# A cross-attention block on one core: six products by seven blocks each, summed in chains in PSUM

## The chip, the cores and the metric

The kernel runs on one core of a Trainium2 chip. Its engines work side by side, each on its own queue in order: TensorE (PE) multiplies matrices into PSUM, an accumulator memory of eight banks of 512 numbers in each of 128 partitions; VectorE (DVE), ScalarE (ACT) and GpSimd (POOL) work element by element; SyncE (SP) here issues DMA transfers. The metric is the device time of one launch in microseconds, lower is better.

## The reference

128 sequences of 128 tokens with 256 features attend to a context of the same shape, with 16 heads of 16 features. Cut to what matters:

```python
q = (query @ Wq + bq); k = (key @ Wk + bk); v = (values @ Wv + bv)     # per head
scores = einsum('bhqd,bhkd->bhqk', q, k) / sqrt(16)
scores = where(j < i, scores, -1e30)             # key j before query i
attn = softmax(scores); attn[:, :, 0, :] = 0
x = layer_norm(query + (attn @ v) @ Wo + bo, ln1_g, ln1_b)
ffn = relu(x @ W1 + b1) @ W2 + b2                # 256 -> 1024 -> 256
out = layer_norm(x + ffn, ln2_g, ln2_b)
```

All of it is in 32-bit floating point. A matmul of that type is two instructions of the chip, each with its weight load.

## The kernel before

The 128 sequences go through in 64 pairs, 256 tokens a pair. A software pipeline, written out by hand, works on several pairs in one step: `step(p)` (L1475) holds the scores and exponentials of pair p, the queries and keys of p + 1, the weighting and output projection of p - 2, the first feed-forward product of p - 3 and the second one of p - 4, and the last normalisation of p - 5. Steps 2 to 6 have functions of their own (`third` to `sixth`), which fill the pipeline; steps 7 to 63 call `step`, and the lines from L1564 on drain it. The order in the code is the order of each engine's queue.

TensorE's part of a step, in its order: the weighting of values by probabilities in `weigh` (L534: 48 small matmuls at L544 and L554), the scores (L410), then four projections of 256 columns: queries (L270), attention output (L573), keys (L270) and values (L325). Each is four matmuls, so eight chip instructions. Then come the second feed-forward product (`second_by_seven`, L864) and the first (`hidden_by_seven`, L1450, of `Hidden`, L957), each split into two halves of its rows and columns and formed from seven block products in place of eight, after Winograd's form of Strassen's scheme. That takes sums of the input blocks (GpSimd, L859 to L862 and L952 to L955) and of the weight blocks (once, ahead), and gives products that are added up by VectorE (L903 to L926, L1002 to L1016). Each product by seven has 28 matmuls of 128 columns. `empty` puts TensorE instructions that do nothing behind a block; the second feed-forward product has 22 of them.

The low scores (queries 0 to 63 of a sequence) go to banks 6, 7, 4 and 5 and are masked into SBUF by `mask` (L419); the high ones stay in banks 0 to 3 and are masked in place (`mask_high`, L816). ScalarE takes the exponential head by head (L839) with the sum of each row as a second result. The sums' inverses are multiplied into the probabilities on GpSimd (`divide`, L482). The probabilities are then transposed in blocks of 32 x 32 on VectorE (`turn`, L491), and 16 transfers (`bring`, L504) carry the blocks to their partitions. The normed tokens are transposed likewise (`turn_x1`, L739) and go through DRAM in five transfers (`across`, L240). The buffers for probabilities, transposed blocks and carried blocks are four of one kind (`wide`, L358).

## Time and profile before

| | us |
|---|---|
| median of three runs | 1484.22 (1484.1 to 1484.62) |
| span of the profiled execution | 1482.7 |
| TensorE busy in it | 1475.0 |
| VectorE busy | 1386.3 |
| GpSimd busy | 1376.5 |
| ScalarE busy | 1324.1 |
| DMA | 204.63 MB, mean 138 GB/s |

The granted clock of TensorE is 0.999 over the span. Busy time counts overlapping instructions of an engine once; an instruction's length in the rows runs from its start to its end, and the next one can start before that end. A row of the chain of waits is a stretch of the chain that ended last; a row of the timeline is a run of like instructions, with the idle time of the engine before it and what released it in square brackets.

### The profile page before, as it was taken

How to read it: one execution, taken by the hardware profiler on the slowest of the kernel's cores; microseconds unless marked ns; L12 is line 12 of the kernel's file. 1: busy time of each engine (PE TensorE's matmuls, PEld its weight loads, DVE VectorE, ACT ScalarE, POOL GpSimd, SP SyncE). 2: the span in 40 equal slices, each digit the busy share in tenths (PEclk: the TensorE clock that was granted, in tenths of full speed). 3: DMA queues.
4: the chain of work that ended last, by engine and by line, in shares of the span. 5: the costliest groups of instructions: out<-in, count | busy, mean ns of one | idle time of the engine just before them, and what ended most of it. 6: DMA issues, size and time to landing. Idle time of an engine off the chain costs nothing.

```text
span 1482.7 us, 53916 instructions
## 1 busy us (share of the span) xinstructions
PE 1475.0 (99%) x19367; PEld 1378.1 (93%) x19367; DVE 1386.3 (93%) x2444; ACT 1324.1 (89%) x5272; POOL 1376.5 (93%) x1530
## 2 busy tenths in 40 slices
PE   9999999999999999999999999999999999999998
PEld 7788999999999999999999999999999999999998
DVE  7999999999999999999999999999999999999977
ACT  6668999999999999999999999999999999999963
POOL 6979999999999999999999999999999999999987
PEclk9999999999999999999999999999999999999999
DMA  8366666555655566665556556566655666555451
GB/s 201 79 133 150 148 150 141 127 146 138 154 144 133 138 146 138 149 144 130 144 132 156 146 128 143 144 137 150 145 132 141 136 153 148 128 141 131 109 137 51
DMA packets 415317, 204.63 MB, mean 138 GB/s; under 512 B 282448, under 2 KB 383056, under 8 KB 415056
## 3 DMA queue, kind: packets, MB, share of 16 engines
q1 hardware_dynamic: 412768, 199.34, 57.5%
q8 instruction: 160, 2.62, 0.8%
q10 hardware_dynamic: 2288, 1.85, 0.5%
q14 instruction: 101, 0.83, 0.2%
HBM read 70.26 MB, written 33.29 MB: 70 GB/s over the span
## 4 chain that ended last, share of the span: by engine, by line
PE 96%; DVE 2%; POOL 1%; ACT 0%; issue 0%; DMA 0%; POOLq 0%; DVEq 0%
PE banks L878 25%; PE banks L990 25%; PE banks L270 15%; PE banks L573 7%; PE banks L325 7%; PE banks L410 6%; PE banks L554 4%; PE banks L544 2%; PE banks L778 2%; PE banks L1042 0%; PE banks L797 0%; DVE su L468 0%; POOL sm L446 0%; PE banks L527 0%; POOL sm L470 0%
## 5 line engine op out<-in xcount | busy, mean ns | idle before, releaser
L839 ACT ACTIVATE sm<-banks,nmx 128x128 f32<-128x128 f32 x944 | 329.8, 377 | 16.3 <-DVE nmx L823 8.7
L485 POOL TENSOR_TENSOR sm<-sm,rs 128x1024 f32<-128x1024 f32 x171 | 322.6, 1901 | 0.0
L839 ACT ACTIVATE sm<-sm,nmx 128x64 f32<-128x64 f32 x944 | 312.5, 368 | 0.0
L497 DVE STREAM_TRANSPOSE tb<-sm 128x1024 f32<-128x1024 f32 x186 | 229.8, 1237 | 17.1 <-DMA pT<-tb 6.9
L1021 ACT ACTIVATE hT<-hT,b1e_c 128x256 f32<-128x256 f32 x464 | 198.1, 497 | 34.7 <-DVE hT L1009 21.0
L839 ACT ACTIVATION_READ_ACCUMULATOR sm<-sm,nmx 128x1 f32 x912 | 201.6, 221 | 0.0
L839 ACT ACTIVATION_READ_ACCUMULATOR sm<-banks,nmx 128x1 f32 x912 | 197.3, 216 | 0.0
L990 PE MATMUL banks<-xS,w1t 128*128 128x128 f32 x1392 | 174.4, 275 | 0.0
L878 PE MATMUL banks<-wt,hS 128*128 128x128 f32 x1440 | 170.7, 275 | 0.0
L878 PEld LDWEIGHTS banks<-wt,hS 128*128 128x128 f32 x1440 | 165.6, 192 | 0.1
L990 PEld LDWEIGHTS banks<-xS,w1t 128*128 128x128 f32 x1392 | 164.8, 192 | 0.0
L823 DVE TENSOR_REDUCE nmx<-banks 128x4 f32<-128x512 f32 x177 | 153.9, 869 | 6.0
L270 PE MATMUL banks<-xT,wq 128*128 128x256 f32 x504 | 125.4, 392 | 0.0
L315 ACT ACTIVATE kT<-banks,bkh,half 128x256 f32<-128x256 f32 x252 | 122.5, 590 | 2.8 <-PE banks L270 2.8
L990 PE MATMUL banks<-x1T,w 128*128 128x128 f32 x944 | 124.6, 275 | 0.2 <-DMA x1T<-x1t 0.2
L573 PE MATMUL banks<-wo,cxT 128*128 128x256 f32 x512 | 121.2, 379 | 0.0
L325 PE MATMUL banks<-wv,cT 128*128 128x256 f32 x512 | 121.0, 379 | 0.0
L270 PE MATMUL banks<-cT,wk 128*128 128x256 f32 x504 | 119.4, 380 | 0.1
L878 PEld LDWEIGHTS banks<-w,hT 128*128 128x128 f32 x944 | 114.7, 192 | 3.1
L990 PEld LDWEIGHTS banks<-x1T,w 128*128 128x128 f32 x944 | 114.9, 192 | 0.4 <-issue 0.3
L878 PE MATMUL banks<-w,hT 128*128 128x128 f32 x944 | 115.2, 275 | 0.0
L573 PEld LDWEIGHTS banks<-wo,cxT 128*128 128x128 f32 x512 | 97.0, 190 | 13.5 <-ACT cxT L566 0.3
(191 smaller groups left out, 3954.1 us busy)
## 6 DMA issues: line engine op xcount, KB each, us to landing
pT<-tb SPq DMA_DIRECT2D x976, 96.0 KB, 2.2
x1t<-tbx SPq DMA_DIRECT2D x252, 64.0 KB, 2.4
x1T<-x1t SPq DMA_DIRECT2D x63, 256.0 KB, 3.0
out_dram<-t SPq DMA_DIRECT2D x63, 256.0 KB, 3.1
xb<-in_x_dram SPq DMA_DIRECT2D x124, 128.0 KB, 3.7
cb<-in_ctx_dram SPq DMA_DIRECT2D x124, 128.0 KB, 4.2
x<-in_x_dram SPq DMA_DIRECT2D x31, 512.0 KB, 5.3
w<-in_L_xattn_W_dram SPq DMA_DIRECT2D x2, 1024.0 KB, 8.3
```

Of the source, the lines that this page charges most:

```text
L270: nc.tensor.matmul(ps[:, m * TP : (m + 1) * TP], w[:, k, m * P : (m + 1) * P], src[:, k, :], start=(k == 0), stop=(k == KC - 1),)
L315: nc.scalar.activation(st["kT"][:, m, e, :], pk[:, m * TP : (m + 1) * TP], AF.Identity, bias=bkh[:, m, e : e + 1], scale=half[:, e : e + 1],)
L325: nc.tensor.matmul(pv[:, s * D : (s + 1) * D], st["cT"][:, k, s * P : (s + 1) * P], wv[:, k, :], start=(k == 0), stop=(k == KC - 1),)
L410: nc.tensor.matmul(st["sps", hi][r][s * HP : (s + 1) * HP, m * 2 * n : (m + 1) * 2 * n].rearrange("p (e j) -> p e j", e=2), st["qT"][strip ...
L485: nc.gpsimd.tensor_tensor(sm[:, part, :], sm[:, part, :], st["rs", hi][:, part, None].to_broadcast([P, part.stop - part.start, sm.shape[2] ...
L497: nc.vector.transpose(st["tb"][:, :, at : at + 256].rearrange("p j (n a) -> p n j a", a=32), st["sm", hi].rearrange("p h j -> p (h j)")[:, ...
L573: nc.tensor.matmul(po[:, s * D : (s + 1) * D], cxT[:, k, s, :], wo[:, k, :], start=(k == 0), stop=(k == KC - 1),)
L823: nc.vector.tensor_reduce(st["nmx", 1][:, 4 * first : 4 * (first + n)], ps, AX.X, ALU.max, negate=True,)
L839: nc.scalar.activation(sm[:, h, :], src, AF.Exp, bias=nmx[:, h : h + 1], scale=1.0, **({"accum_out": st["su", hi][:, h : h + 1]} if summed ...
L878: nc.tensor.matmul(out, left(k), right(k), start=(k == 0), stop=(k == FC // 2 - 1))
L990: nc.tensor.matmul(ps[:, i * P : (i + 1) * P].rearrange("p (n a) -> p n a", a=32), left(i), right, start=True, stop=True,)
L1021: nc.scalar.activation(self.hT[:, f], self.plains.get(f, self.hT[:, f]), AF.Relu, bias=b1e_c[:, f : f + 1], scale=1.0,)
```

## The change

All six products of a step are now formed from seven blocks: queries, keys, values and attention output too, each with 7 matmuls of 128 columns (14 chip instructions) for the 4 of 256. Their input sums are made on GpSimd (`cc` for the context, which keys and values share, `xc` for the tokens, `oc` for the attention's context), the weight sums once in steps 5 and 6.

The seven blocks are summed in PSUM. A product has three accumulators of one bank (`a`, `b`, `f`; three banks for the first feed-forward product). Blocks 1, 2 and 5 start them; a reader on ScalarE or VectorE takes `a` and `f` out; blocks 6 and 3 are added onto `a` and `f`, a reader takes them out; then 7 onto `a`, a reader; then 4 onto `a`, a reader. A block is so held up until the reader ahead of it is through.

The probabilities are no longer divided on GpSimd. The inverses of the sums are transposed, each repeated 16 times (`turn_inverse`), and multiplied into the context where VectorE takes it out of PSUM, which ScalarE did before. One set of 16 transfers carries probabilities, inverses and the normed tokens of another pair; the way through DRAM goes in the steady steps. The buffers `turned` and `brought` are single, the probabilities' own (`wide`) too.

The step is a list of 151 names, `ORDER`, in place of nested calls; each engine takes its own names of it in that order. A name with -1 or -2 is run one or two passes later than its pair's other names: with -1 stand both feed-forward products (`w`, `h`) with nearly all that belongs to them, the low probabilities' and the inverses' turn; with -2 the rectifiers of the even hidden blocks (`re`), the odd ones' too (`ro`), and one half of the residual. Two passes are added behind step 62 to drain these, and `last_step` follows. `EMPTY` says how many empty TensorE instructions stand behind each group of blocks, 2 to 5. A pass has 768 TensorE instructions with its weight loads. The last normalisation is of pair p - 6. In steps 5 and 6 exponentials have their sums as second results, the weight sums of the projections are made, and the normed tokens and inverses are turned.

Names of the list that the next part uses: `weigh`, `scores`, `context`; `maskB3`, `maskB2`, `maskA` for the low scores, `add0` to `add3` and `max0` to `max3` for the high ones, one bank each; `eh` and `el` exponentials of two heads, high and low; `turn0` to `turn2` and `turni`; `o1` to `o4`, `v`, `q`, `k`, `w`, `h` the groups of blocks in a chain; `ok`, `oa`, `or` and the like their readers.

The diff, cut to its core:

```diff
-    def inverse(p, hi):
-        st = states[p]
-        rs = st["rs", hi] = small.tile([P, H], F32, tag=f"rs{hi}", name=f"rs{hi}_{p}")
-        nc.vector.reciprocal(rs, st["su", hi])
-
-    def divide(p, hi, part):
-        st = states[p]
-        sm = st["sm", hi]
-        nc.gpsimd.tensor_tensor(
-            sm[:, part, :], sm[:, part, :],
-            st["rs", hi][:, part, None].to_broadcast([P, part.stop - part.start, sm.shape[2]]),
-            ALU.mult,
-        )
+    def reciprocals(p):
+
+        st = states[p]
+        rs = st["rs"] = small.tile([P, 2 * H], F32, tag="rs", name=f"rs_{p}")
+        nc.vector.reciprocal(rs, st.pop("su"))
+
+    def turn_inverse(p):
+
+        st = states[p]
+        nc.vector.transpose(
+            turned[:, :, WIDTH : WIDTH + P].rearrange("p j (n a) -> p n j a", a=32),
+            st.pop("rs").rearrange("p (n g) -> p n g", n=4)[:, :, :, None].to_broadcast(
+                [P, 4, HH, DK]
+            ),
+        )
...
-    def bring(p, queue, which):
...
+    def bring(p, queue, which, whole=False):
+
+        blocks(p)
+        at = slice(p % 2 * P, p % 2 * P + ROW) if whole else slice(P, P + WIDTH)
         for u in which:
             i, j = u // NS, u % NS
             queue.dma_start(
-                st["pT whole"][32 * j : 32 * j + 32, i, :], st["tb"][32 * i : 32 * i + 32, j, :]
-            )
+                brought_all[32 * j : 32 * j + 32, i, at],
+                turned_all[32 * i : 32 * i + 32, j * ROW + at.start : j * ROW + at.stop],
+            )
...
+        if "inv" in states[p]:
+            parts = "p (m s l q a) -> p m s l q a"
+            pc = states[p].pop("pc").rearrange(parts, m=KC, s=2, l=2, q=2)
+            to = cxT.rearrange("p m s (l q a) -> p m s l q a", l=2, q=2)
+            inv = states[p].pop("inv")
+            nc.vector.tensor_tensor(
+                to[:, :, :, :, 1], pc[:, :, :, :, 1], inv[:, :, :, :, 1], ALU.mult
+            )
+            for l in range(2):
+                at = slice(1 - l, 32)
+                nc.vector.tensor_tensor(
+                    to[:, :, :, l, 0, at], pc[:, :, :, l, 0, at], inv[:, :, :, l, 0, at], ALU.mult
+                )
+            return
...
+    class Seven:
+
+        def __init__(self, at, data, sums, weights, mixed, turned=False, depth=1):
+            self.at, self.turned, self.depth = at, turned, depth
+            self.factors = {
+                1: (data(0, 0), weights(0, 0)), 2: (data(0, 1), weights(1, 0)),
+                5: (sums(0), mixed(0)), 6: (sums(1), mixed(1)), 3: (sums(3), weights(1, 1)),
+                7: (sums(2), mixed(2)), 4: (data(1, 1), mixed(3)),
+            }
+            self.name = f"pb{turns[0]}"
...
+        def run(self, *which):
+            for n in which:
+                out = self.of({2: 1, 5: 2, 3: 2}.get(n, 0))
+                left, right = self.factors[n]
+                if self.turned:
+                    left, right = right, left
+                for k in range(self.depth):
+                    nc.tensor.matmul(
+                        out, left(k) if self.depth > 1 else left,
+                        right(k) if self.depth > 1 else right,
+                        start=(n == 1 and k == 0), stop=(k == self.depth - 1),
+                        skip_group_check=True,
+                    )
...
+    class Onto(Seven):
+
+        def onto(self, t, base):
+            self.t = t.rearrange("p s (h d) -> p (s h) d", h=2)
+            self.base = base.rearrange("p s (h d) -> p (s h) d", h=2)
+
+        def join(self, to, src, of):
+            nc.vector.tensor_tensor(to, src, of, ALU.add)
+
+        def keep(self):
+            self.join(self.t[:, ::3], self.two(0, 2), self.base[:, ::3])
+
+        def keep2(self):
+            self.join(self.t[:, 1], self.a, self.base[:, 1])
+
+        def add(self):
+            self.join(self.t[:, 3], self.a, self.t[:, 3])
+
+        def add2(self):
+            self.join(self.t[:, :2], self.two(1), self.t[:, :2])
+
+        def rest(self):
+            self.join(self.t[:, 2], self.a, self.base[:, 2])
...
+    class First:
...
+        def run(self, *which):
+            raw = lambda s, k: self.x1T[:, s, :, k, :]
...
+                ps = self.banks[{2: 1, 5: 2, 3: 2}.get(n, 0)]
+                for i in range(NI):
+                    nc.tensor.matmul(
+                        ps[:, i * P : (i + 1) * P].rearrange("p (n a) -> p n a", a=32),
+                        left(i), right, start=(n in (1, 2, 5) and i == 0), stop=True,
+                        skip_group_check=True,
+                    )
...
+    KINDS = {
+        "V": (Values, 4), "O": (Attention, 5), "Q": (Queries, 7), "K": (Keys, 3),
+        "W": (Second, 6), "first": (First, 0, 2),
+    }
...
-    def hidden_by_seven(p):
-
-        h = Hidden(p - 3)
-        h.run(1)
-        h.run(6)
-        h.keep()
-        values_out(p)
-        h.u2()
-        h.run(7)
...
+    ORDER = """
+        weigh re0-2 res1-2 turn2-1 re2-2 re3-2 re1-2 context norm2-1 scores hs2-1 turni-1 vs-1
+        maskB3 br2 add0 oc0 o1 ro0-2 maskB2 oc2 maskA ro2-2 finish1-1 v1 ro3-2 max0 ro1-2 q1 ok
+        vk0 eh1 oc1 lowmax w1-1 hs0-1 qk br3 w2-1 vk1 add1 eh0 xs2-1 max1 el6 v2 hs1-1 stats2
+        w5-1 eh3 add3 oc3 h2-1 eh2 max3 br1 hs3-1 wk-1 vk2 el5 o2 tokc-1 v3 eh7 xc2-1 h1-1 ok2
+        add2 xc3-1 eh6 max2 cc0 q2 res0 vf el4 o3 br0 va w3-1 ob hk-1 oa vb eh4 cc1 w6-1 hb-1
+        xs0-1 el0 cc2 o4 k1 wk2-1 xs1-1 qk2 or tokx el7 finish2-1 load w7-1 stats1 eh5 q3 means
+        v4 kk h6-1 qa xc0 wb-1 el1 cc3 qb k2 deviations vr el3 wa-1 h5-1 turn1 kk2 loadx hk2-1
+        w4-1 xs3-1 store-1 norm1 turn0 addbo k3 h7-1 hk5-1 ka kb el2 xc1 turnx q4 k4 h3-1 ha-1
+        kr qr h4-1 ks recip ks2 hf-1 wr-1
+    """.split()
...
+    EMPTY = {'w1': 5, 'h1': 4, 'w2': 5, 'h2': 5, 'w3': 5, 'h3': 4, 'w4': 5, 'h4': 5, 'w5': 5, 'h5': 4, 'w6': 5, 'h6': 5, 'w7': 4, 'h7': 5, 'v1': 3, 'o1': 2, 'q1': 2, 'k1': 3, 'v2': 2, 'o2': 2, 'q2': 3, 'k2': 2, 'v3': 2, 'o3': 3, 'q3': 2, 'k3': 3, 'v4': 2, 'o4': 2, 'q4': 3, 'k4': 2}
...
+    LEAD = {}

     def step(p):
-        last = p == NP - 1
+
+        empty(LEAD.get(p, 0))
+        for key in ORDER:
+            key, late = (key.split("-") + ["0"])[:2]
+            q = p - int(late)
+            if FIRST <= q < NP - 1:
+                OPS[key](q)
+                if key in EMPTY:
+                    empty(EMPTY[key])
+
+    FIRST = 7
+
+    def last_step(p):
...
+    late = max(int((key + "-0").split("-")[1]) for key in ORDER)
+    for p in range(FIRST, NP - 1 + late):
         step(p)
+    last_step(NP - 1)
```

More of the change, by code (lines that the diff above doesn't have):

```diff
@@ L1475, in step, with combine_one @@
-    def step(p):
-        last = p == NP - 1
+        inverse(p)
+        turn_x1_blocks(p - 2)
+    def combine_one(p, which, data, n):
+        st = states[p]
+        if which not in st:
+            st[which] = soft.tile([P, 4, P], F32, tag=which, name=f"{which}_{p}")
+        c = st[which]
+        left, right, how = {
+            0: (data(1, 0), data(1, 1), ALU.add), 1: (c[:, 0], data(0, 0), ALU.subtract),
+            3: (data(0, 1), c[:, 1], ALU.subtract), 2: (data(0, 0), data(1, 0), ALU.subtract),
+        }[n]
+        nc.gpsimd.tensor_tensor(c[:, n], left, right, how)
@@ new lines, in at_x1, with combine_x1_one @@
+    def at_x1(p):
+        return lambda s, k: states[p]["x1T"][:, s, :, k, :]
+    def combine_x1_one(p, n):
+        st = states[p]
+        if "xS" not in st:
+            st["xS"] = ffn.tile([P, 4, NS, 32], F32, tag="xS", name=f"xS_{p}", bufs=1)
+        c, data = st["xS"], at_x1(p)
+        left, right, how = {
+            0: (data(1, 0), data(1, 1), ALU.add), 1: (c[:, 0], data(0, 0), ALU.subtract),
+            3: (data(0, 1), c[:, 1], ALU.subtract), 2: (data(0, 0), data(1, 0), ALU.subtract),
+        }[n]
+        nc.gpsimd.tensor_tensor(c[:, n], left, right, how)
@@ L1496, in step @@
         exponential_by_head(p, 1, TWOS, True)
-        if not last:
-            mask(p, 0, A)
         low_maximum(p)
-        if not last:
-            exponential_by_head(p, 0, range(H), True)
-            queries(p + 1)
         attention_out(p - 2)
```

646 lines of the change are left out of this document (507 added, 139 removed).

## The prediction

> **What bounds the kernel now.** I read the page first: the span, the busy shares, the chain that ended last, the DMA issues. TensorE is busy 99% of the span, and the chain consists of it; but VectorE, GpSimd and ScalarE are at 93, 93 and 89%, so hardly anything lies behind TensorE.
>
> ```profile
> span 1482.7 us, 53916 instructions
> PE 1475.0 (99%) x19367; PEld 1378.1 (93%) x19367; DVE 1386.3 (93%) x2444; ACT 1324.1 (89%) x5272; POOL 1376.5 (93%) x1530
> PE 96%; DVE 2%; POOL 1%; ACT 0%; issue 0%; DMA 0%; POOLq 0%; DVEq 0%
> L485 POOL TENSOR_TENSOR sm<-sm,rs 128x1024 f32<-128x1024 f32 x171 | 322.6, 1901 | 0.0
> pT<-tb SPq DMA_DIRECT2D x976, 96.0 KB, 2.2
> ```
>
> Then the chain of waits in order of time, cut to one steady step (start, length, what):
>
> ```profile
> 704.16 0.36 PE banks L544 x16
> ...
> 705.64 1.55 PE banks L410 x45
> 707.19 1.92 PE banks L270 x8
> ...
> 712.57 1.73 PE banks L325 x8
> 714.29 6.25 PE banks L878 x56
> 720.55 6.25 PE banks L990 x56
> 726.80 0.36 PE banks L544 x16
> ```
>
> A step is 726.80 - 704.16 = 22.64 us, all TensorE: weights times values 1.48 (to 705.64), scores 1.55, four 256-column projections of 1.73 (the first 1.92, as the issue stalls 0.19 behind the scores), and two products by seven of 6.25. A projection is 8 chip instructions of 1.73 / 8 = 0.216; a product by seven has 56 of 6.25 / 56 = 0.1116.
>
> **The change: TensorE.** Each projection becomes seven blocks of 128 columns, 14 chip instructions, 14 x 0.1116 = 1.56 in place of 1.73. The new step has 1.48 + 1.55 + 4 x 1.56 + 12.5 = 21.8 us of TensorE work. That is 0.86 below 22.64, 0.67 if the 0.19 stall behind the scores stays. Chaining the sums in PSUM costs the array nothing that shows: 128-column matmuls into a region that accumulates (L878) and into one that doesn't (L990) both take 6.25 for 56.
>
> The Trainium skill, "TensorE: Matmul & The Clock Gate", section "Back-to-back issue gap", speaks against narrow matmuls: weight load and matmul set the pace together, with 81 ns at 128 columns and 131 at 512. An estimate between these gives 98 at 256; in that proportion 14 narrow instructions would cost 14 x 0.18 = 2.5 us, 0.8 more than a projection now. The rows differ (0.1116 against 0.216), and the measurement decides.
>
> The empty instructions are at most 5 behind 8 matmuls, or 3 behind 2. Before, L878 carries 22 of them and takes what L990 takes without any. In the warm-up, 24 stood among the first 8 matmuls shown here:
>
> ```profile
> 14.47 1.89 PE L270 MATMUL banks<-xT,wq 128*128 128x256 f32 x8
> ...
> 723.96 1.06 PE L990 MATMUL banks<-x1T,w 128*128 128x128 f32 x8
> ```
>
> They span 1.89 with the last one's tail, against 1.73 from start to start in a steady step. I cost the empty ones at nothing; what hides them is the array time of the matmuls queued ahead.
>
> **VectorE** is where the change is paid: it reads the chains in small pieces, scales the context, and turns the inverses. Its timeline gives the price of each kind as the distance to the next start:
>
> ```profile
> 704.11 1.25 DVE L497 STREAM_TRANSPOSE tb<-sm 128x1024 f32<-128x1024 f32 x1
> 705.28 1.18 DVE L1016 TENSOR_TENSOR hT<-hT,banks 128x1024 f32<-128x1024 f32 x1
> 706.38 0.75 DVE L434 TENSOR_TENSOR sm<-banks,neg 128x256 f32<-128x256 f32 x2
> 707.05 0.42 DVE L820 TENSOR_TENSOR banks<-banks,neg 128x256 f32<-128x256 f32 x1
> 707.51 0.69 DVE L823 TENSOR_REDUCE nmx<-banks 128x4 f32<-128x512 f32 x1
> 708.12 0.42 DVE L820 TENSOR_TENSOR banks<-banks,neg 128x256 f32<-128x256 f32 x1
> ...
> 714.70 0.22 DVE L480 RECIPROCAL rs<-sa 128x16 f32<-128x16 f32 x1
> 714.84 0.66 DVE L256 STREAM_TRANSPOSE xT<-xb 128x512 f32<-128x512 f32 x1
> 715.42 0.67 DVE L256 STREAM_TRANSPOSE cT<-cb 128x512 f32<-128x512 f32 x1
> 716.01 0.39 DVE L586 BATCH_NORM_STATS2 bs<-t 128x6 f32<-128x256 f32 x1
> ...
> 722.46 0.69 DVE L1002 TENSOR_TENSOR hT<-hT,banks 128x512 f32<-128x512 f32 x1 [0.15 <-ACT hT L999]
> ...
> 724.16 0.69 DVE L1006 TENSOR_TENSOR hT<-hT,banks 128x512 f32<-128x512 f32 x1 [0.20 <-PE banks L990]
> 724.76 0.71 DVE L742 STREAM_TRANSPOSE tbx<-x 128x512 f32<-128x512 f32 x1
> ```
>
> Out of PSUM, 512 columns cost 0.60 (724.16 to 724.76) and 256 cost 0.335 (two from 706.38 to 707.05); on that line 128 columns, not in this step, cost 0.20. The big transpose is 1.17, a 512-column one 0.58, a maximum 0.61, statistics 0.31 (0.39 less the 0.08 by which neighbours overlap), a small one 0.14. An instruction that needs the one before it costs more: 0.46 from 707.05 to 707.51, 0.125 over 0.335. Counted off the new step's list:
> - 4 of 512 columns (mask A, three hidden sums): 2.40
> - 14 of 256 (two masks, four mask additions, seven chain reads, one half of the context): 4.69
> - 16 of 128 (the other chain reads, the rest of the context): 3.20
> - 3 mask additions right ahead of their maximum: 0.38
> - 4 maxima 2.44; the low maximum, 1024 columns like L1016, 1.10
> - transposes: 3 x 1.17, and four of 512 columns (two inputs, inverses, normed tokens) at 0.58: 5.83
> - 4 statistics 1.24, 4 means and the reciprocal 0.70
>
> The sum is 22.0 us: more than TensorE's 21.8. The inverses' transpose, which repeats each number 16 times, and the context's five-level pattern are in no trace; I take them as their nearest rows, at worst as the next larger (0.6 and 0.3 more). VectorE now starts 0.20 after TensorE's end (723.96 to 724.16), and loses such 0.20 and 0.15 in a step. Behind the last hidden block it must wait so again; I add 0.3. **A step becomes 22.3 us, paced by VectorE, 0.34 less than now.**
>
> **GpSimd and ScalarE** stay behind that. GpSimd loses three divisions of 1.9 (L485) and one of two sets of small ones; it gains twelve 128-column sums and one 512-column spread:
>
> ```profile
> 708.28 1.27 POOL L859 TENSOR_TENSOR hS<-hT 128x512 f32<-128x512 f32 x1 [0.36 <-ACT hT L1021]
> ...
> 713.32 0.47 POOL L952 TENSOR_TENSOR xS<-x1T 128x128 f32<-128x128 f32 x1
> ```
>
> That is 12 x 0.47 + 1.27 = 6.9 against 5.7 and a set: about even. ScalarE gives the context and half the spreading of keys away and takes smaller pieces of the chains; its exponentials stay.
>
> SP's sixteen transfers grow from 96 to 128 KB and land within 2.2 us now; they replace five transfers through DRAM a step, are issued over the first half, and are needed by the next step. Costed at nothing; if that cover were gone, the next step's first matmul would wait.
>
> **Filling and draining** cost something that the steady step doesn't show. The two products by seven of a step are now run one pass later (marked -1). So the first pass has only 1.48 + 1.55 + 6.25 = 9.3 us for TensorE, but ScalarE's full row of exponentials:
>
> ```profile
> 708.31 0.37 ACT L839 ACTIVATE sm<-banks,nmx 128x128 f32<-128x128 f32 x1
> ...
> 713.98 0.38 ACT L839 ACTIVATE sm<-sm,nmx 128x64 f32<-128x64 f32 x1
> ...
> 719.28 0.86 ACT L296 ACTIVATE qT<-banks,bqs_c 128x256 f32<-128x256 f32 x2
> ...
> 723.63 1.09 ACT L625 ACTIVATE x<-t,nb,sd 128x256 f32<-128x256 f32 x2
> ...
> 726.08 1.71 ACT L1021 ACTIVATE hT<-hT,b1e_c 128x256 f32<-128x256 f32 x4 [0.37 <-DVE hT L1009]
> ```
>
> They begin when the context, four masks or additions and the first maximum are through: 1.68 + 0.74 + 2.2 = 4.6 us. Then 16 + 16 heads take 719.28 - 708.31 = 11.0, and the copies and the normalisation (1.0) between them some 3.4, an estimate from L296's 0.86 for two pieces of 256: 19 us, when keys are ready for the next scores, which stand 1.5 behind the start of their pass. The first pass takes about 17.7. The pass after the last full one has just the two products, 12.5 us, but their chains alone: the second block waits for seven rectifiers (0.41 each), a normalisation and the copies (4.8 us in, against 2.5 if unhindered), the third for GpSimd's sum behind them (6.2), and later waits of 0.3 to 0.5 come twice. About 17.7 again. So the 56 steps 7 to 62 become 55 full passes and these two, which hold 35.4 us in the place of one step: 12.8 us extra. In the two steps ahead, ScalarE now reads out a sum behind each of 32 heads, between nothing and 3 us a step on an engine that waits there; I take 1 us in all.
>
> So 55 passes gain 55 x 0.34 = 18.7 us and 13.8 go: 4.9 us less, a span of 1478. The median of 1484.2 stands 1.5 above the span: **1479 us.**
>
> **Rivals.** *The chains' readers make TensorE wait (slower).* The first output block (bank 5) waits for mask B3 of the low scores in that bank, and this stands on VectorE behind a rectifier, the 1.17 transpose, the context and the inverses' turn: 0.34 + 1.17 + 0.74 + 0.58 + 0.42 = 3.25 after the last hidden block. TensorE then has 92 matmuls up to the output's last block, 10.27; 0.20 later VectorE reads that, and has 8.5 us of its list left to the next rectifier. The circle takes 22.2 by these rows, as long as VectorE's own work; each late piece in it lengthens it, and behind the waiting block stand all of TensorE's products. At 22.55 the steady part gains 4.9 and loses 13.8: 1493 us. It decides from 22.39 on, where the gain of 55 x 0.25 is eaten by filling and draining. For it: every reader stands within 0.3 us of its block. Against: before, TensorE lost nothing to readers. The Trainium skill bears on it: "PSUM — Partial Sum Buffer", section "PSUM bank collisions raise a hardware error", wants PSUM guarded by bank and quadrant, not by address, so that a reader of one third of a bank bars TensorE from the rest. No row here shows such a read.
>
> *TensorE keeps the pace.* If small VectorE pieces overlap better than 0.20, a step is 21.8 to 22.0: 55 x 0.75 - 13.8 = 27 us less, 1457. For it: 0.14 for a reciprocal. Against: 22.0 of VectorE work.
>
> *Nothing is left.* At 22.4 the gain equals fill and drain: 1484.
>
> **How the numbers follow.** My forecast (22.2 to 22.35, 1474 to 1482) has 0.44; the waiting readers (22.45 and more, 1487 to 1500) 0.30; TensorE's pace 0.14; nothing left 0.12. A measurement of this kernel can tell about 0.2%, 3 us. Faster: TensorE's pace and nearly all of the forecast, 0.55. Same: 0.15 from the case between and the forecast's edge. Slower: 0.30. The range for 8 in 10 goes from 1460 to 1497, the forecast's own from 1474 to 1482.
>
> **What would show it.** In the changed trace: passes of 22.3 us; VectorE with idle time only behind the last hidden block; 128-column reads 0.20 apart; projections of 14 at 0.1116; a first pass and a drained pass of some 18 us each. TensorE idle before the first output block, released by the low mask, beyond 0.5 us in each pass would show the first rival. Wrong would be transfers as releasers of TensorE, or GpSimd ahead of VectorE.

## The result and the profile after

The changed kernel takes 1507.21 us (median, 1505.33 to 1508.16) against 1484.16 for the kernel before: the ratio is 1.0151, 95% interval 1.0137 to 1.0166. It is slower by 23 us (1.5%), where the forecast was 5 us less.

The page of the changed kernel first: span, busy shares, the engines' shares of the chain that ended last, and two groups with the idle time ahead of them.

```profile
span 1506.2 us, 62177 instructions
PE 1478.2 (98%) x20711; PEld 1405.8 (93%) x20711; DVE 1418.2 (94%) x3397; ACT 1294.9 (86%) x5445; POOL 1317.1 (87%) x1877
PE 32%; DVE 29%; SPq 16%; POOL 7%; ACT 7%; DMA 5%; issue 4%; DVEq 0%; POOLq 0%; ACTq 0%
L428 PEld LDWEIGHTS banks<-kT,qT 32*64 32x64 f32 x3840 | 90.0, 132 | 31.2 <-ACT hT L1433 17.2
L1433 ACT ACTIVATE hT<-banks,b1e_c 128x256 f32<-128x256 f32 x168 | 67.4, 472 | 50.9 <-DVE hT L1431 50.9
```

Before, the chain was TensorE to 96%. Now it goes round: TensorE, VectorE, ScalarE, GpSimd and SP's queue each have a part. A chain that changes engines several times in a pass is a circle of waits. The scores' weight loads (L428) wait 17.2 us in all for ScalarE's rectifiers (L1433), and those wait 50.9 us for VectorE's one rectifier (L1431).

Where the time went is seen by cutting the span at the first matmul of each `weigh` (L574). The windows view gives, for each stretch, its length, the busy time of each engine with the count of instructions, TensorE's granted clock, and DMA. The stretches here are step 5, step 6, the first two passes of the list (7 and 8), a steady pass, pass 62 with the drained pass, and the last step:

```profile
99.33:117.49 18.16, 17.64 (x225) 14.89 (x225) 14.70 (x23) 15.05 (x73) 17.50 (x23) 1.00 0.64 136
117.49:142.98 25.49, 22.25 (x241) 18.06 (x240) 19.11 (x32) 22.47 (x95) 16.80 (x27) 1.00 0.67 137
142.98:163.42 20.44, 14.72 (x217) 12.58 (x216) 16.50 (x43) 15.22 (x78) 8.77 (x18) 0.72 0.73 151
163.42:188.01 24.59, 24.59 (x328) 23.66 (x328) 22.04 (x54) 18.42 (x84) 19.87 (x30) 0.88 0.58 124
727.90:750.38 22.48, 22.41 (x329) 21.70 (x328) 22.11 (x56) 20.74 (x90) 20.53 (x31) 1.00 0.70 152
1380.33:1422.33 42.00, 38.15 (x441) 36.40 (x440) 27.69 (x67) 26.95 (x104) 31.49 (x41) 0.96 0.27 64
1422.33:1447.07 24.74, 22.25 (x265) 19.43 (x265) 19.15 (x38) 19.48 (x85) 14.40 (x21) 0.93 0.43 98
```

| stretch | before, us | after, us | difference |
|---|---|---|---|
| up to step 5 | 99.56 | 99.33 | -0.23 |
| step 5 | 17.12 | 18.16 | +1.04 |
| step 6 | 21.52 | 25.49 | +3.97 |
| 7 and 8 | 45.28 | 45.03 | -0.25 |
| 9 to 61, each | 22.635 | 22.49 | 53 x -0.14 = -7.3 |
| 62 and the drained pass | 22.63 | 42.00 | +19.37 |
| last step | 19.90 | 24.74 | +4.84 |
| behind it | 57.01 | 59.13 | +2.1 |

The sum is +23.5, the difference of the spans. So the steady passes did get shorter, by less than half of the forecast, and the two ends cost 31 us instead of 14. The clock fell to 0.72 in pass 7, and below 1.00 in pass 8 and at the end.

The chain of one steady pass (start, length, what), from one rectifier of VectorE to the next:

```profile
728.12 0.48 DVE hT L1431
...
728.63 1.21 ACT hT L1433 x3
...
729.89 1.59 PE banks L428 x48
731.48 5.35 PE banks L1175 x46
...
739.28 2.47 PE banks L1175 x22
...
741.78 0.52 DVE t L1327 x2
...
749.95 0.55 DVE hT L1417
...
750.61 0.48 DVE hT L1431
```

750.61 less 728.12 is 22.49, the pass. The even rectifiers empty banks 0 and 1, VectorE's one first, then ScalarE's three; only then can the scores go into those banks; then come 90 instructions of blocks up to `w6` without a gap, 10.27 us. VectorE, idle for 0.15 us ahead of it, reads `w6` (741.78), then `o4`, the last output block, and works off its list without a pause up to the next rectifier. VectorE's timeline has the read of `w6` (the x1b in it belongs to the second feed-forward product) and the first low mask, `maskB3`:

```profile
730.99 0.38 DVE L452 TENSOR_TENSOR sm<-banks,neg 128x256 f32<-128x256 f32 x1
...
741.78 0.29 DVE L1327 TENSOR_TENSOR t<-banks,x1b 128x128 f32<-128x128 f32 x1
```

`maskB3` ends at 731.37, 0.1 us before the blocks start (731.48): a second circle, through this mask, is almost as long. VectorE is busy for 22.11 of the 22.48 us, TensorE for 22.41. By the busy shares either could be the limit.

At the start, the chain in step 6 and pass 7 hangs on the transfers. SP issues them one behind the other; these rows are the landings of the last one of a set, and what starts behind it:

```profile
133.32 2.45 DMA brought<-turned
...
135.91 7.14 PE banks L858 x32
...
156.20 2.32 DMA brought<-turned
...
158.99 2.37 DVE turned L521 x2
```

In the chain a transfer of SP's queue (SPq) mostly takes 0.60 and 0.04 to the next, so a set is 16 x 0.64 = 10.2 us of issuing and 2.4 to land. The hidden layer of step 6 starts behind it, and so does VectorE's next transpose into the buffer that the set reads.

### The profile page after: what moved, and what is told of

It is laid out like the page before. It is cut to its first block, busy times and chain, and to the rows that moved or that the text cites. A ratio compares the mean times of both kernels' runs of the same rounds, so it can differ in the third digit from the quotient of the medians.

```text
span 1506.2 us, 62177 instructions
## 1 busy us (share of the span) xinstructions
PE 1478.2 (98%) x20711; PEld 1405.8 (93%) x20711; DVE 1418.2 (94%) x3397; ACT 1294.9 (86%) x5445; POOL 1317.1 (87%) x1877
## 3 DMA queue, kind: packets, MB, share of 16 engines
q8 instruction: 188, 3.08, 1.0%
## 4 chain that ended last, share of the span: by engine, by line
PE 32%; DVE 29%; SPq 16%; POOL 7%; ACT 7%; DMA 5%; issue 4%; DVEq 0%; POOLq 0%; ACTq 0%
PE banks L1175 19%; SPq L540 15%; DVE turned L521 9%; PE banks L1392 5%; ACT hT L1433 4%; PE banks L428 4%; DMA brought<-turned 3%; DVE hT L1411 2%; POOL kT L1272 2%; POOL hS L1868 2%; DVE t L1327 2%; DVE hT L1431 2%; DVE bsa L1900 1%; DVE kr L1259 1%; DVE xT L277 1%
## 5 line engine op out<-in xcount | busy, mean ns | idle before, releaser
L521 DVE STREAM_TRANSPOSE turned<-sm 128x1024 f32<-128x1024 f32 x186 | 222.5, 1222 | 6.0 <-DMA brought<-turned 4.2
L1868 POOL TENSOR_TENSOR hS<-hT 128x512 f32<-128x512 f32 x112 | 142.9, 1276 | 30.5 <-ACT hT L1433 29.6
L428 PE MATMUL banks<-kT,qT 32*64 32x256 f32 (+1 forms) x3840 | 123.7, 335 | 6.2 <-DVE t L1446 0.8
L428 PEld LDWEIGHTS banks<-kT,qT 32*64 32x64 f32 x3840 | 90.0, 132 | 31.2 <-ACT hT L1433 17.2
L1392 PE MATMUL banks<-brought,w 128*128 128x128 f32 x896 | 118.3, 275 | 0.0
L1433 ACT ACTIVATE hT<-banks,b1e_c 128x256 f32<-128x256 f32 x168 | 67.4, 472 | 50.9 <-DVE hT L1431 50.9
L1392 PEld LDWEIGHTS banks<-brought,w 128*128 128x128 f32 x896 | 109.2, 192 | 0.0
L1421 ACT ACTIVATE hT<-hT,b1e_c 128x256 f32<-128x256 f32 x224 | 95.6, 497 | 0.7
L1873 DVE TENSOR_TENSOR banks<-banks,neg 128x256 f32<-128x256 f32 x224 | 94.0, 420 | 0.2
L691 ACT ACTIVATE x<-t,nb,sd 128x256 f32<-128x256 f32 x126 | 69.0, 596 | 23.7 <-POOL nb L1919 12.0
```

The lines of the kernel that those rows point to most:

```text
L428: nc.tensor.matmul(st["sps", hi][r][s * HP : (s + 1) * HP, m * 2 * n : (m + 1) * 2 * n].rearrange("p (e j) -> p e j", e=2), st["qT"][strip ...
L521: nc.vector.transpose(turned[:, :, at : at + 256].rearrange("p j (n a) -> p n j a", a=32), states[p]["sm", hi].rearrange("p h j -> p (h j) ...
L1392: nc.tensor.matmul(ps[:, i * P : (i + 1) * P].rearrange("p (n a) -> p n a", a=32), left(i), right, start=(n in (1, 2, 5) and i == 0), stop ...
L1421: nc.scalar.activation(self.hT[:, f, at], self.hT[:, f, at] if src is None else src, AF.Relu, bias=b1e_c[:, f : f + 1], scale=1.0,)
L1433: nc.scalar.activation(out, src, AF.Relu, bias=bias, scale=1.0)
L1868: nc.gpsimd.tensor_tensor(c[:, n], left, right, how)
```

## The experiments

They stand in the order in which the theories fell. Times are medians of four runs, which spread by up to 7 us (e3) and mostly by 1 to 5; the kernel before, run beside each group, took 1484.1 to 1484.4 us each time. A pass is the median of those from 9 to 60, and "holes" is what these passes take above their median in all.

**The circle, first attempt: e1 to e4.** e1 puts one mask earlier, e2 moves VectorE's rectifier to ScalarE, e3 does both, e4 leaves out the empty instructions.

```diff
-   scores hs2-1 turni-1 vs-1 maskB3 br2
+   scores hs2-1 maskB3 turni-1 vs-1 br2                      # e1, e3
-   relu_even(n, n == 0)
+   relu_even(n, False)                                       # e2, e3
-   EMPTY = {'w1': 5, 'h1': 4, ...}
+   EMPTY = {}                                                # e4
```

> Edit: in the list of a pass maskB3 (VectorE frees the scores' bank 5) goes ahead of turni (VectorE's transpose of the inverses). VectorE's work is the same. Theory T (the pace of 22.49 us a pass is a circle: VectorE's first rectifier, turn2, turni, maskB3, then o1 to o4 on TensorE, then VectorE's last read of them and the rest of its list): maskB3 ends 0.62 us earlier, so o1 and all behind it may; VectorE has about 0.25 us of waits a pass to lose, so 22.49 becomes 22.25 to 22.35 and the kernel gets 8 to 13 us faster than the changed kernel. Rival R1 (VectorE's own instructions fill the pass, the waits are a by-product): no change, within 2 us. Rival R2 (the 16 transfers and the loads behind them on SP's queue set it): no change either, within 2 us.

> Edit: the rectifier of blocks 0 (re0) goes from VectorE to ScalarE beside the three others. It takes 0.39 us of work from VectorE in each pass and the wait of ScalarE's three rectifiers for VectorE's one (0.9 us a pass). Theory T: TensorE's scores wait less and the circle through maskB3 is shorter by the rectifier's 0.39 us, 0.25 to 0.4 us a pass, 13 to 22 us in all. Rival R1 (VectorE's own work): the whole 0.39 us a pass, 20 us; it and T part only in whether VectorE has waits left (T: yes, 0.2 us a pass or more at o4's last read). Rival R2 (SP's queue): within 2 us of the changed kernel.

> Edit: both of the above. Theory T: TensorE's own 21.8 to 22.0 us or VectorE's 22.0 less 0.39 is what is left to pace a pass: 21.9 to 22.1 us, 20 to 32 us faster than the changed kernel. R1: the same 20 us as the rectifier alone. R2: nothing.

> Edit: the empty instructions behind each block of a pass on TensorE's queue are left out (106 a pass), nothing else. The prediction cost them at nothing: within 2 us of the changed kernel. [...]

| | us | a pass | holes |
|---|---|---|---|
| changed kernel | 1507.2 | 22.49 | 0.6 |
| e1 | 1526.3 | 22.81 | 2.5 |
| e2 | 1512.5 | 22.44 | 7.5 |
| e3 | 1517.4 | 22.55 | 9.0 |
| e4 | 1514.9 | 22.54 | 6.7 |

All four were slower than the changed kernel; none of the expected times came. (The expectations speak of 106 empty instructions; the trace has 104 a pass.) The chains say why. In e1:

```profile
818.50 0.60 SPq L540
...
819.14 2.45 DMA brought<-turned
821.59 0.04 DVEq L521
```

Here 16 transfers and a landing are the pass's chain. `turni` stands 0.64 us later behind the rectifier, the first transfer starts 0.15 us after its end as in the changed kernel, and the next transpose (L521) waits for the last one. From `turni` (807.80) to the transpose that waits for the last transfer (822.24) it is 14.4 us. In e2, from a normal pass and then from a longer one:

```profile
749.98 0.17 DVE cxT L600
...
750.32 0.47 DVE cxT L605 x2
750.79 0.40 DVE turned L504
...
751.34 0.39 DVE sm L452
...
751.77 5.40 PE banks L1175 x46
...
884.15 0.21 PE banks L584 x12
884.36 1.03 issue
885.39 0.55 PE banks L584 x20
```

The rectifiers have left the chain. In their place it goes from the last matmuls of `weigh` to VectorE's context, to `turni`, to `maskB3` and to `o1`, then through TensorE's blocks back to `weigh`: 22.44 us. That refutes R1: 0.39 us of VectorE's work went, and 0.05 came. In e3 the same circle is longer, since `maskB2`, which the values' bank waits for, now stands behind `turni`. So three circles lie close together (22.49, 22.44, and the transfers' some 0.3 us below in the changed kernel), and to open one shows the next. The second quote shows something else: TensorE stops for 1.03 us amid 32 like matmuls, and no engine releases it.

**Opening two circles, and the ends: e5 to e8.**

```diff
-   turn2-1 re2-2 re3-2 re1-2 context norm2-1 scores hs2-1 turni-1
+   turn2-1 turni-1 re2-2 re3-2 re1-2 context norm2-1 scores hs2-1   # e5, with e2's edit
-   bring_all(p - 1, EVERY)
+   bring_all(p - 1, EVERY[:12])                                     # e6: steps 5, 6, last
+   bring_all(p - 1, EVERY[12:], nc.scalar)
-   hidden(p - 3, range(FC), ...)                                    # e7, in step 6
+   if p == FIRST and key in PAIRS:                                  # e7, at w2, h2, h1, h6
+       f, b = PAIRS[key]
+       hidden(p - 4, range(f, f + 2), None, (b,) * 4)
```

> Edit: all four rectifiers of the even blocks on ScalarE, as in e2, and turni (the transpose of the inverses) goes ahead of the context's reads on VectorE, where VectorE waited 0.22 us for the context's matmuls. Theory after e1 to e4 (three circles of nearly one length: rectifiers to scores 22.49; TensorE's 20.55 us from o1 round to the context's matmuls plus VectorE's context, turni and maskB3 22.44; turni to the 16 transfers to turn1 and back to turni 22.2, 22.8 where turni is put later): the first is gone as in e2, the second loses 0.3 us since turni lies beside the matmuls, the third loses 0.4 us since the transfers start earlier; a pass takes 22.05 to 22.2 us, 12 to 20 us less than e2's kernel in all, less what TensorE's holes with no releaser take (7 us in e2). Rival (a pass is filled by something that none of the edits moves, since e2 alone brought 0.05 us): 22.4 us, within 2 us of e2's.

> Edit: in the steps written out by hand (step 5, step 6 and the last step) 4 of the 16 transfers of a set are issued by ScalarE instead of SP, so that a set is issued in some 7.9 instead of 10.8 us. Theory (SP's issue of 16 transfers one behind the other, 0.64 us each, and 2.4 us to land, is what the hand-written steps wait for): the last step's first hidden block waits 2.4 us less and keeps its clock (1.8 us), step 6 gets 1.4 to 2.9 us shorter: 4 to 8 us in all. Rival (other waits in those steps end right behind these, on ScalarE's exponentials): under 2 us, or slower by the 2.2 us that ScalarE issues in each of the steps. The passes in between stay at 22.49 us.

> Edit: the plain hidden layer of pair 3 (32 matmuls, 7.1 us) leaves step 6 and goes in four parts into the holes of the first pass of the list, where the skipped blocks of the two hidden products would stand. Theory (the fill costs what it does because the first pass has waits of TensorE that nothing fills, 8 us of them, and pass 8 starts at half clock behind them): steps 6 to 8 together get 4 to 8 us shorter. Rival (SP's set of 16 transfers paces steps 6 and 7, TensorE's holes are a by-product): step 6 gets shorter by the 1.4 us wait and what stands behind it, pass 7 longer by as much; within 2.5 us in all. The other passes stay at 22.49 us.

> Edit: the edits of e5, e6 and e7 together. Theory: the sum of the three, 25 to 40 us under the changed kernel, 1467 to 1482 us: level with the kernel before or faster by up to 1 %. Rival (the passes stay at 22.4 us): 1490 to 1500 us.

e5: 1505.2 us, a pass 22.355 and 4.5 us of holes: less than hoped, but better than e2 by 7.3 us, and the page's chain is now of TensorE:

```profile
PE 90%; DVE 2%; ACT 2%; POOL 2%; SPq 1%; issue 1%; DMA 1%; POOLq 0%; DVEq 0%; ACTq 0%
```

22.355 us is 18.75 for 168 instructions of 0.1116 (four projections of 14, two products of 56), 1.48 for `weigh`, 1.93 for the scores and 0.2 of seams. The scores are 0.4 above the 1.55 of the kernel before; no wait on another engine is shown ahead of them in the steady passes, and the cause stays open.

e6: 1506.3 us, no gain that can be told. The last step got 3.59 us shorter and step 6 1.36, as the theory has it; but the drained pass got 1.06 longer, the step behind the last one 1.50 and the tail 1.0. The rival has it: at the end another chain stands right behind.

e7: 1518.6 us. Step 6 got 5.5 us shorter, pass 7 got 17.2 longer. Its chain alternates between the moved blocks and ScalarE:

```profile
151.06 1.74 PE banks L858 x8
...
152.82 0.84 ACT hT L865 x2
...
153.82 2.07 ACT sm L920 x12
...
155.93 2.01 PE banks L858 x8
```

ScalarE takes its work in order. The rectifiers of the moved blocks stood among the exponentials, the exponentials waited for the rectifiers, and the rectifiers for TensorE. e8, with all edits: 1511.7 us, a miss for the same reason; its pass 7 takes 37.4 us.

**What paces e5, the holes, and the first pass: e9 to e12.** e9 takes the attention output back to plain blocks, e10 doubles the empty instructions, e11 puts idle matmuls into the first pass, e12 combines. e9 computes the same; the idle matmuls of e11 and e12 add results that nobody reads.

```diff
-   "o1": lambda p: of(p - 2, "O").run(1, 2, 5),      # e9; o2 to o4, oc, oa, or ... left out
+   "o1": lambda p: attention_out(p - 2),
-   empty(EMPTY[key])
+   empty(2 * EMPTY[key])                              # e10
+   if p == FIRST and key in WARM:                     # e11, e12: 12 groups of 8 matmuls
+       warm_up(WARM[key])
-   for key in ORDER:                                  # e12: DRAIN has norm2-1 and vs-1
+   for key in ORDER if p < NP - 1 else DRAIN:         # behind ro1-2 instead of ahead of ro0-2
```

> Edit: e5's kernel with the attention output back to its plain eight blocks (8 matmuls over 256 columns and one read of 0.6 us on VectorE, instead of 14 over 128 columns, five reads of 1.3 us and GpSimd's four combinations). Theory (in e5 TensorE itself paces a pass: 18.75 us of blocks, 1.46 of weigh and context, 2.1 of scores; VectorE has 0.3 us to spare): the pass gets longer by the 1.73 less 1.56 = 0.17 us, 22.5 us, 9 us more in all, though VectorE has 0.7 us less to do. Rival (VectorE and its reads still pace e5): 0.3 us a pass or more less, 22.05 us, 16 us faster than e5.

> Edit: e5's kernel with twice the empty instructions behind each block (212 a pass). Question: the holes of TensorE with no releaser (4.5 us in e5, 7.3 in e2, 6.6 in e4 without empties, 0.4 in the changed kernel). Theory (TensorE's sequencer outruns what is fetched for it, and the empties hold it back): fewer holes, 0 to 2 us, passes still 22.36 us, 2 to 4 us faster than e5. [...]

> Edit: the changed kernel, and in its first pass of the list 12 groups of 8 matmuls over 128 columns, whose results nobody reads, stand where the skipped blocks of the two hidden products would (0.9 us of TensorE each at full clock). Theory (the first pass is paced by the readers of the chains and by the transfers; its holes let the clock fall, and pass 8 starts at half clock for that: weigh, context and scores 4.8 us instead of 3.3): pass 7 stays within 0.7 us of 20.4, pass 8 gets 1 to 2 us shorter, 23 us instead of 24.6. Rival (pass 8 is long because its transfers and the loads behind them come late, whatever the clock): pass 8 stays at 24.6, and pass 7 gets longer by what TensorE has no holes for.

> Edit: e5's kernel with the transfers of step 6 split as in e6, the matmuls of e11 in the first pass, and in the drained pass ScalarE's rectifiers of the odd blocks ahead of its norm2 and the copies of the values. Theory: e5 less 1.4 (step 6), 1 to 2 (pass 8) and 1.7 us (in the drained pass TensorE waits for the last rectifier, which stands behind 1.7 us of other work of ScalarE): 1499 to 1502 us. It does not reach the 1484 us of the kernel before: TensorE's 22.36 us a pass save 0.28 us x 53 = 15 us, and the ends still cost 25 us or more. Rival (what is taken from the ends comes back behind, as in e6): 1504 to 1507 us.

1560.3, 1534.6, 1557.0 and 1548.0 us: four misses, of 30 to 50 us each. Two things came together. The first is e9's alone; even its undisturbed passes take 23.18:

```profile
780.04 1.94 PE banks L617 x8
...
782.07 0.70 DVE t L665
...
782.83 0.81 ACT sm L920 x4
...
793.40 0.53 ACT kr L1243 x2
...
793.97 0.38 PE banks L1175
```

VectorE waits at the one big read (L665) until all eight instructions are done; behind it in VectorE's order stand the low maximum and three of the high ones, behind these ScalarE's exponentials, and behind those its copy of the keys, which TensorE waits for. It says nothing on what a plain product costs TensorE: the edit made a new circle.

The second thing concerns all. e11's passes take 23.2 us, though from pass 9 on it holds the same instructions in the same order as the changed kernel. The page lists DMA queues of the kind "instruction": q8 moved 188 packets in the changed kernel, 3.08 MB in all, so 16.4 KB each. In the steady pass above the DMA view shows three of them, and TensorE's queue holds 328 matmuls, 328 weight loads, 8 waits and these empty instructions:

```profile
q8 instruction: 3, 0.05, 0.9%
```

```profile
L240 PEldq NOP  x104: 13/13/13, 731.7 to 749.5; - x104
```

That is 768 = 3 x 256. A packet so holds 256 instructions and begins at the same place of every pass. Counted likewise, e2, e3 and e5 have 767 a pass (a wait on a semaphore had gone), e4 664, e9 749, e10 871; e11 has 768, moved by 384, one and a half packets. In e9 the place drifts through the whole packet, with nothing else changing from pass to pass. With the place taken as the count of instructions ahead of a pass modulo 256, 26 passes that begin at 253 to 123 take 23.17 to 23.24 us, and 26 that begin at 124 to 250 take 23.18 to 24.35, 23.67 on average. e4 shows the same: 22.50 on average against 22.85. The changed kernel stands at 73.

The traces say more: the holes stand at the packets' edge. Number TensorE's instructions from the first one in the trace. In the passes 9 to 60 of all versions, `weigh` and the scores have 231 holes of over 0.25 us that no engine ends, and each of them stands ahead of instruction 193 or 194 modulo 256. In the changed kernel this edge falls into `weigh`, and there is no such hole. In e11, e12 and e14, and in the slower half of e9's passes, it falls among the scores or close to them, and the holes are there (in 51 of 52 passes of e14). In e5 it moves on through `weigh` by one instruction a pass; holes come from pass 36 on. So an edge in these two parts can cost time and need not. (Of 17 more such holes, outside these two parts, one is at 193; the others are near 0.) e10 answers its question as well: twice the empties leave the holes, and no pass is under 22.58 us.

**The packets, and what can be had: e13 to e16.**

```diff
-   'k4': 2}
+   'k4': 3}                        # e13, e16: with e5's edits, 768 again
-   LEAD = {}
+   LEAD = {7: 128}                 # e14: 128 empty instructions once; e15, e16: 64
-   for i in range(8):
+   for i in range(4):              # e15, e16, in warm_up
```

> Edit: e5's kernel with one empty instruction more behind the last block of the keys, so that a pass has 768 TensorE instructions again (e5 has 767, since one of the waits on a semaphore is gone) and the packets of 256 instructions fall on the same place in each pass, the place they have in the changed kernel. Packet theory: no holes, all passes 22.36 us, 4 to 5 us faster than e5: 1500 to 1501 us. Rival (the holes belong to a pass in which TensorE has no wait left): 3 us or more of holes again, 1504 to 1506 us.

> Edit: the changed kernel with 128 empty instructions on TensorE's queue once, in front of the first pass of the list; nothing else. All later instructions stand half a packet of 256 further back, as in e11. Packet theory: a pass takes 22.9 to 23.3 us instead of 22.49, as in e11, with a hole at the scores that nothing releases; 25 to 40 us slower than the changed kernel, 1532 to 1547 us, for some 2 us of empty instructions. Rival (e11 was slow for its matmuls in the first pass): 1507 to 1510 us and 22.49 us a pass.

> Edit: e11 with 4 matmuls in each of the 12 groups instead of 8 (e11's took 1.79 us a group, twice what was meant, since each matmul of these is two instructions of 0.1116 us) and 64 empty instructions in front of the first pass, which makes 256 instructions more, a whole packet. Packet theory: the passes are at 22.49 us again. Theory of the clock: pass 7 takes 20.4 to 21.5 us though it holds 10.7 us of matmuls more, pass 8 22.4 to 23.0 instead of 24.59: 1 to 2 us faster than the changed kernel in all, 1505 to 1506 us. Rival (pass 8 is long for its transfers): pass 8 stays above 24 us, 1507 us or more.

> Edit: e12's kernel (rectifiers on ScalarE, turni early, split transfers in step 6, matmuls in the first pass, the drained pass's rectifiers first) with 768 instructions a pass and the shift made a whole packet as in e13 and e15. Packet theory: the passes at 22.36 us with no holes: e13 less 1 to 2 us (fill) and 1 to 3 us (step 6, drained pass): 1496 to 1499 us, still slower than the kernel before. Rival: the passes have holes again, 1505 us or more.

e14 is the clearest run of the study: 1552.9 us, ratio 1.0466 (1.0451 to 1.0482), for empty instructions at one place. A pass takes 23.2 us, as in e11; on average 0.69 more than in the changed kernel, and 53 times 0.69 is 37 us. At the 128 empties themselves TensorE stands still for 6.85 us, not the 2 expected: in the trace one empty instruction starts 0.071 us behind the other. On the page the scores' weight loads wait twice as long as in the changed kernel, 28.4 us of it for no engine; below it the chain shows one such hole:

```profile
L428 PEld LDWEIGHTS banks<-kT,qT 32*64 32x64 f32 x3840 | 96.7, 132 | 62.0 <-issue 28.4
```

```profile
731.58 1.07 PE banks L428 x15
732.66 0.43 issue
733.08 1.13 PE banks L428 x17
```

`weigh` and the scores hold 160 of a pass's 328 matmuls in 3.5 of its 22.5 us. Where a packet has to come among the scores, TensorE mostly stops. The Trainium skill, "Runtime: NRT & Kernel Launch", section "Instruction fetch mechanics", says that instructions come in blocks of 16 KiB (256 instructions) and that going from one block to the next is mostly hidden. The packets' size agrees; going on is hidden in the changed kernel, not in e14, where a pass takes 0.69 us more.

e13: 1499.2 us, 6 us under e5 for one empty instruction a pass; 22.35 us a pass, 0.8 us of holes. The packet theory holds, but only 3.8 us of the 6.4 between the two profiles lie in the passes; 1.9 lie in the last step, where TensorE's clock stayed up in e13 and not in e5 (see the end).

e15: 1512.2 us. The passes are at 22.49 again. Passes 7 and 8 by the windows view:

```profile
145.00:168.76 23.76, 22.53 (x313) 21.17 (x313) 16.89 (x43) 14.63 (x76) 8.71 (x17) 0.93 0.64 135
168.76:191.53 22.77, 22.46 (x330) 21.79 (x330) 21.57 (x54) 18.39 (x84) 19.79 (x30) 1.00 0.63 130
```

Pass 8 went from 24.59 to 22.77 at full clock: the excess was the clock's, as the theory says. But pass 7 took 3.3 us more, and the 64 empties in front of it 2.0; it doesn't pay. e16: 1502.0, a miss, for the same reason (with pass 7 at 23.1 and step 6 at 27.7); its drained pass is 2.5 us shorter, its last step 1.7 longer.

**The last two: e17, e18.** e17 is the changed kernel with e5's edit of `turni` alone; e18 is e13 with the reordered drained pass and the last step's transfers split.

> Edit: the changed kernel with turni ahead of the context's reads, the rectifiers as they are (one on VectorE, three on ScalarE behind it). Circle theory (the circle through the rectifiers and the scores sets 22.49 us and does not hold turni): 22.47 to 22.49 us a pass, within 2 us of the changed kernel. Rival (VectorE's waits are what counts, wherever they go): 22.35 to 22.42 us, 4 to 7 us faster.

> Edit: e13's kernel (22.36 us a pass, no holes), with ScalarE's odd rectifiers first in the drained pass (as in e12 and e16, where it gave 2.5 us and the last step took 1.7 back) and 4 of the 16 transfers of the last step issued by ScalarE (as in e6, where it gave 3.6 us and the steps behind took 2.6 back). If both keep what is not taken back: 1496 to 1498 us. If the end is one chain that waits elsewhere: 1498 to 1501 us, no faster than e13. Either way slower than the kernel before.

e17: 1521.3 us, a pass 22.75, a miss. With VectorE's rectifier still there, `turni` pushes the context's reads back, and the scores wait for these too, as the idle times ahead of L428 show:

```profile
  ACT hT L1433: 17.1, 54
  DVE cxT L605: 8.7, 54
```

8.7 / 54 = 0.16 us of the 0.26 that a pass got longer. The context is read out of bank 7, into which low scores are written next; the changed kernel has no such row. So the circle through the scores does hold the context, and e5's edit is good only with e2's.

e18: 1497.0 us, the fastest of all versions (ratio to before 1.009, 1.0073 to 1.0107; e13's interval overlaps it). The drained pass is 2.5 us shorter than e13's and the last step 1.5, while what is behind takes 1.5 back. No version reached the kernel before.

## Why the prediction was wrong

Of the 28 us between 1479 and 1507, 11 are the steady passes' and 17 the ends'.

**"A step becomes 22.3 us, paced by VectorE, 0.34 less than now."** The saving was 0.14 (53 x 0.14 = 7.3 us, not 18.7). The prices were good: narrow reads are 0.20 apart, 14 matmuls take 14 x 0.1116, and VectorE's busy time is 22.11 against a sum of 22.0. What failed is the pacing. VectorE's list is nearly full, but the pass closes through ScalarE's rectifiers and the scores. e2 and e5 show it: 0.39 us less on VectorE gave 0.05, and only when the context's circle was opened too did it come to 22.355. There TensorE itself sets the pass, so its own sum, 21.8, was 0.55 too low as well: 0.4 of it are the scores (1.93, not 1.55), the rest seams between blocks.

**The first rival** (the readers make TensorE wait: 22.45 and more) had the size of the steady pass, and nearly its circle: from the rectifier to TensorE's blocks, to VectorE's list and back. Its link was `maskB3`; the link that closes it in the changed kernel is the wait of the scores for the four rectifiers, whose first holds up the other three. `maskB3`, which ends there 0.1 us before the scores do, is the link in e2. Its total, 1493, was too low for the ends, which it shared with the forecast.

**"Filling and draining"**: 13.8 us forecast; with 55 steady passes counted as there, 23.5 + 55 x 0.14 = 31.2 measured. By its own terms: the first two passes were to take 17.7 + 22.3 = 40, and took 45.0, since pass 7's chain is one set of transfers for 12.9 us (145.61 to the landing at 158.52) and the clock falls (e15: 1.8 of it is the clock of pass 8; in e5 and e13, at a clock of 0.95, pass 8 takes 23.3). Steps 5 and 6 were to cost 1 and cost 5.0. The drained pass was to take 17.7 and took 19.5. The last step and what follows had no term, and cost 6.9; 1.7 of it is the clock in the last step's hidden layer. That is where the time went; edits show why only for pass 8 (e15), the drained pass (e18) and the transfers of step 6 and the last step (e6).

**SP's transfers "costed at nothing"** held in the steady pass, with 0.3 us to spare: e1 moved their start by 0.64, and the pass became 0.32 longer. In pass 7 and in the steps written by hand it didn't hold; e6 took 3.59 from the last step and 1.36 from step 6 by issuing four transfers elsewhere, though the end gave most of it back.

**"I cost the empty ones at nothing"** is right as a price in the steady pass (without them it is no shorter, e4), and misses what they do: they make a pass three whole packets, so that the packets' edge keeps its place (e4, e13, e14). It isn't why the changed kernel is slower, as that has 0.6 us of holes. The 2 us that e14's expectation gives for 128 of them are in no run.

What stays open: the end of the kernel was taken apart only in part (e6, e18), why the scores got 0.4 us longer, why an edge in `weigh` costs time in some passes and not in others, and why the clock at times stays up over the same wait.

## To carry to other kernels

When five queues are each near the pace, look for circles rather than for the fullest engine: follow the chain from one instruction to the same one a pass later, and list the next circle before opening the first. A software pipeline that is made one or two passes deeper must earn its fill and drain, price every step written by hand, with its transfers. And before comparing variants of a long unrolled loop, count each engine's instructions per pass: a variant that changes the count or the place of the code also changes where its instruction packets fall, which here was worth 37 us, more than most edits.

## What the hardware showed that was not expected

- One shift of TensorE's code by half a packet of 256 instructions made each pass 0.69 us longer on average (e14); a pass of 767 instructions instead of 768 cost 3.8 us in the passes (e5 against e13).
- Empty instructions start 0.071 us apart. Behind queued matmuls the 104 of a pass cost nothing, but where TensorE had nothing else, it stood still for 6.85 us at 128 of them (e14), for 1.98 and 0.91 at 64 (e15, e16).
- Waits of little over 2 us go with a lower clock. Ahead of the last step's hidden layer TensorE waits 0.5 to 3.3 us in the changed kernel and e1 to e18. After the seven waits of up to 2.1 us that layer's 32 matmuls took 7.08 us, from the first one's start to the next matmul behind them; after ten of the twelve waits of 2.2 us and more they took 8.76. The two others are e12 (2.3 us) and e13 (2.7 us). The changed kernel, where the granted clock of the last step is 0.93, and e13:

```profile
1438.31 8.83 PE L858 MATMUL banks<-brought,w 128*128 128x256 f32 x32 [2.40 <-DMA brought<-turned]
```

```profile
1428.86 2.47 DMA brought<-turned
...
1431.97 7.14 PE banks L858 x32
```
